# Pairwise bilinear products on one core: x transposed in pairs of fields, one buffer for 384 pairs of w, and another split of x loads between two DMA queues

## The chip, the cores and the metric

One core of a Trainium2 chip runs the kernel. The metric is the device time of one execution in microseconds (us); lower is better. Five runs of the kernel before gave 1345.14 to 1346.18 us, median 1345.78 us.

## The reference

`x` is (4096, 32, 64) in float32: 4096 samples of 32 fields with 64 numbers each. `W` is (496, 64, 64): one 64 x 64 matrix for each of the 496 pairs of fields (i, j) with i < j.

```
idx_i, idx_j = np.triu_indices(32, k=1)
vi, vj = x[:, idx_i, :], x[:, idx_j, :]
out = jnp.einsum('bpd,pde->bpe', vi, W) * vj        # (4096, 496, 64) float32
```

Field i of a sample is multiplied by the pair's matrix, and the result, element by element, by field j. The output has 520 MB, x has 33.5 MB and W has 8.1 MB.

## The kernel before

**Tiles and blocks.** A block is 256 samples, two to each of the 128 partitions (sample `k` of a partition is 0 or 1). A block has two tiles, one for each `k`, so there are 16 blocks and 32 tiles. A block of x stands in SBUF as one buffer `xs` of 1 + 64 fields to a partition (L71); field 0 is set to zero by GpSimd (L72), so that each field can be transposed with the one ahead of it. There are two such buffers, and x is loaded one block ahead.

**W.** The 496 pairs are loaded in four chunks of 128, 128, 128 and 112 pairs (L113 to L118), reordered by a copy (`order_w`, L120) and transposed on TensorE (`turn_w`, L127). They stay in SBUF as four buffers `wT`, with one half of the output columns on partitions 0 to 63 and the other half on partitions 64 to 127.

**x.** `turn_x` (L138) makes the transposed x of eight fields: eight transposes on TensorE, each of a field with the one ahead of it, into PSUM, and one ScalarE copy of 128 x 1024 to SBUF (L147). A tile needs four of them, and each is put out four steps ahead of the step that first uses it (`AHEAD`, L174).

**Steps.** A step is one field i and up to 16 of its partners j. For each chunk of w that the step touches, two matmuls (L244), one for each half of the output columns and on its own half of the partitions, write PSUM. VectorE then multiplies PSUM by the 16 partners of x (L261) and writes `ot`. For seven values of i ScalarE copies PSUM to `tmp` (L258) and GpSimd multiplies (L259).

**Output.** A tile's 496 pairs are cut in five groups of 90, 97, 99, 105 and 105 pairs. A group is one buffer `ot`, of which there are three, and one transfer on SyncE's queue (L266): 128 rows of 23,040 to 26,880 bytes. The first three tiles go group by group, since w arrives in between; from the fourth on each tile goes through its five groups.

**Loads of x.** Blocks 0 and 1 are loaded on SyncE's queue. For the others the load is put out at the seventh step of the block ahead (L188 to L191), when the last reads of the buffer's old block are done. It goes on ScalarE's queue as one transfer of 128 rows of 16 KB (L76). Blocks 4, 7, 10 and 13 go another way (`load_fifteen`, L95):

- rows 0 to 119 on GpSimd's queue in two transfers of half the fields (L103), with pieces of 4 KB;
- after each of these a small transfer of 17 rows of four bytes (`turn_engines`, L86);
- rows 120 to 127 on ScalarE's queue, in a transfer of five rows and one of three (L99), 16 KB a row.

A transfer of 120 rows on GpSimd's queue takes 15 of the core's 16 DMA engines, and the small one takes the remaining one, so that the next transfer of 120 rows leaves out the same engine. One call of `turn_engines` with five rows at the start sets which engine that is; one with eleven at the end (L270) brings the count back to a multiple of 16.

**Order.** Each engine's instructions run in the order of its queue. The order follows from the loop over the steps and from the dictionaries `due` (transposes and copies) and `loads` (x loads), which the kernel fills ahead of the loop.

Of the kernel before, what the change touches and what calls it, by code (L numbers as in the profile page):

```python
# [8 lines left out]
F32 = mybir.dt.float32  # L9
# [3 lines left out]
def kernel(  # L13
# [16 lines left out]
    nc = tc.nc  # L30

    B, F, D = x.shape
    P = 128
    NB = 2
# [3 lines left out]
    E2 = D // 2  # L38
    BANK = 512
    CH = BANK // E2  # L40
    RUN = 2 * BANK // P
    p0 = [i * (F - 1) - i * (i - 1) // 2 for i in range(F)]


# [7 lines left out]
    wrows = list(zip(cuts[:-1], cuts[1:]))  # L52

    const = ctx.enter_context(tc.tile_pool(name="const", bufs=1))
    xpool = ctx.enter_context(tc.tile_pool(name="xpool", bufs=2))
    xtpool = ctx.enter_context(tc.tile_pool(name="xtpool", bufs=4))
    tpool = ctx.enter_context(tc.tile_pool(name="tpool", bufs=4))
    opool = ctx.enter_context(tc.tile_pool(name="opool", bufs=3))
    psum = ctx.enter_context(tc.tile_pool(name="psum", bufs=4, space=bass.MemoryType.PSUM))

    ident = const.tile([P, P], F32, tag="ident", name="ident")
    make_identity(nc, ident)

    xs = {}

    def rows_of(dram: bass.AP, blk: int) -> bass.AP:
        return dram[blk * NB * P : (blk + 1) * NB * P]

    def new_x(blk: int):

        xs[blk] = xpool.tile([P, 1 + NB * F, D], F32, tag="xs", name=f"xs_{blk}")  # L71
        nc.gpsimd.memset(xs[blk][:, 0, :], 0.0)  # L72

    def load_x(blk: int, eng, k0: int = 0, k1: int = NB):
        src = rows_of(x, blk).rearrange("(p k) f d -> p (k f) d", k=NB)
        eng.dma_start(out=xs[blk][:, 1 + k0 * F : 1 + k1 * F, :], in_=src[:, k0 * F : k1 * F, :])  # L76

# [3 lines left out]
    SWR = 120  # L81
# [4 lines left out]
    def turn_engines(k: int):  # L86
        n = k if k > 1 else 17
        c = used[0] % 8
        used[0] += 1
        src = x[: NB * n].rearrange("(p k) f d -> p k f d", k=NB)  # L90
        tc.keep_in_program_order(
            nc.gpsimd.dma_start(out=scratch[:n, :, c : c + 1], in_=src[:, :, 0, 0:1])  # L92
        )

    def load_fifteen(blk: int):  # L95
        rows = rows_of(x, blk).rearrange("(p k) f d -> p k f d", k=NB)
        dst = xs[blk][:, 1:, :].rearrange("p (k f) d -> p k f d", k=NB)
        for a, b in ((SWR, SWR + 5), (SWR + 5, P)):
            nc.scalar.dma_start(out=xs[blk][a:b, 1:, :], in_=rows[a:b].rearrange("p k f d -> p (k f) d"))  # L99
        for h in range(2):  # L100
            cut = slice(h * F // 2, (h + 1) * F // 2)
            tc.keep_in_program_order(
                nc.gpsimd.dma_start(out=dst[:SWR, :, cut, :], in_=rows[:SWR, :, cut, :])  # L103
            )
            turn_engines(1)


    wflat = w.rearrange("p d e -> p (d e)")
    raw, wT = {}, {}
    EU = 2 * BANK // P  # L110
    NU = E2 // EU

    def load_w(c: int, eng=nc.sync):  # L113

        a, b = wrows[c]
        pool, tag = ((opool, "ot"), (opool, "ot"), (const, "w3"), (const, "w3"))[c]
        raw[c] = pool.tile([P, D * D], F32, tag=tag, name=f"raw_{c}")
        eng.dma_start(out=raw[c][: b - a, :], in_=wflat[a:b])  # L118

    def order_w(c: int, k: int, copy):  # L120
        r = wrows[c][1] - wrows[c][0]
        rp = tpool.tile([P, EU, 2, D], F32, tag="tmp", name=f"rp_{c}_{k}")
        src = raw[c][:r, :].rearrange("p (d h e) -> p e h d", h=2, d=D)
        copy(rp[:r], src[:, k * EU : (k + 1) * EU])  # L124
        return rp

    def turn_w(c: int, k: int, rp, copy):  # L127
        r = wrows[c][1] - wrows[c][0]
        if c not in wT:
            wT[c] = const.tile([P, r, E2], F32, tag=f"w{c}", name=f"wT_{c}")  # L130
        pt = psum.tile([P, EU, P], F32, tag="ps", name=f"ptw_{c}_{k}")
        for n in range(EU):
            nc.tensor.transpose(  # L133
                pt[:, n, :r], rp[:r, n].rearrange("p h d -> p (h d)"), ident[:r, :r]
            )
        copy(wT[c][:, :, k * EU : (k + 1) * EU], pt[:, :, :r].rearrange("p e r -> p r e"))  # L136

    def turn_x(blk: int, k: int, q: int, copy):  # L138

        pt = psum.tile([P, RUN, P], F32, tag="ps", name=f"ptx_{blk}_{k}_{q}")  # L140
        for n in range(RUN):
            s = k * F + q * RUN + n
            nc.tensor.transpose(  # L143
                pt[:, n, :], xs[blk][:, s : s + 2, :].rearrange("p f d -> p (f d)"), ident
            )
        xT = xtpool.tile([P, RUN, P], F32, tag="xT", name=f"xT_{blk}_{k}_{q}")
        copy(xT, pt)  # L147
        return xT


# [8 lines left out]
    first = {}  # L159
# [11 lines left out]
    place = {ts: n for n, ts in enumerate(sched)}  # L171


    AHEAD = 4  # L174
    due: dict = {}
    for t in range(NT):
        for q in range(F // RUN):
            at = place[t, first[q * RUN - 1] if q else 0] - AHEAD
            due.setdefault(max(0, at), []).append(("x", t // NB, t % NB, q))
    for c, orders, turns in (  # L180
# [9 lines left out]
    loads = {place[blk * NB, LATE]: blk + 1 for blk in range(2, NBLK - 1)}  # L190
    loads[place[LEAD, LATE]] = 2  # L191

    new_x(0)
    load_x(0, nc.sync, 0, 1)
    load_w(0)
    load_w(1)
    load_x(0, nc.sync, 1, NB)
    load_w(2)
    new_x(1)
    load_x(1, nc.sync)  # L200
    turn_engines(5)

    v, p, a = nc.vector.tensor_copy, nc.gpsimd.tensor_copy, nc.scalar.copy
    xT, rps = {}, {}
    xT[0, 0, 0] = turn_x(0, 0, 0, a)
    due[0] = [d for d in due[0] if d != ("x", 0, 0, 0)]
    for k, copy in enumerate((v, v, v, a)):
        rps[0, k] = order_w(0, k, copy)
    for k, copy in ((0, a), (3, a), (1, v), (2, a)):
        turn_w(0, k, rps.pop((0, k)), copy)  # L210

    ots = {}
    for s, (t, st) in enumerate(sched):
        blk, kt = divmod(t, NB)
        g, i, c0, m = steps[st]
        if s in loads:
            new_x(loads[s])
            if loads[s] % 3 == 1:
                load_fifteen(loads[s])
            else:  # L220
                load_x(loads[s], nc.scalar)
        for what, *args in due.get(s, ()):
            if what == "x":
                xT[tuple(args)] = turn_x(*args, a)
            elif what == "turn":
                turn_w(*args, rps.pop(tuple(args)), a)
            else:
                c, k = args
                rps[c, k] = order_w(c, k, (v, v, p, v)[c] if k % 2 == 0 else (v, v, p, a)[c])
                if (c, k) == (2, NU - 1):  # L230
                    load_w(3, nc.scalar)

        base, end = groups[g]
        pa = p0[i] + c0
        if pa == base:
            ots[t] = opool.tile([P, cap, D], F32, tag="ot", name=f"ot_{t}_{g}")
        ot = ots[t]
        ps = psum.tile([P, 2, CH, E2], F32, tag="ps", name=f"ps_{s}")
        for c, (lo, hi) in enumerate(wrows):
            lo, hi = max(pa, lo), min(pa + m, hi)  # L240
            if lo < hi:
                for h in range(2):
                    n = i + 1 - h
                    nc.tensor.matmul(  # L244
                        ps[:, h, lo - pa : hi - pa, :],
                        xT[blk, kt, n // RUN][h * D : (h + 1) * D, n % RUN, :],
                        wT[c][h * D : (h + 1) * D, lo - wrows[c][0] : hi - wrows[c][0], :],
                        start=True,
                        stop=True,
                    )  # L250
        o = pa - base
        j = 1 + kt * F + i + 1 + c0
        dst = ot[:, o : o + m, :].rearrange("p m (h e) -> p m h e", h=2)
        src = ps[:, :, :m, :].rearrange("p h m e -> p m h e")
        xj = xs[blk][:, j : j + m, :].rearrange("p m (h e) -> p m h e", h=2)
        if i in aside and c0 == 0 and s not in no_aside:
            tmp = tpool.tile([P, CH, 2, E2], F32, tag="tmp", name=f"tmp_{s}")
            nc.scalar.copy(tmp, src)  # L258
            nc.gpsimd.tensor_mul(dst, tmp, xj)  # L259
        else:  # L260
            nc.vector.tensor_mul(dst, src, xj)  # L261

        ends = (p0[2], end) if s < NS and (t, g) == (0, 0) else (end,)
        if pa + m in ends:
            n0 = p0[2] if len(ends) > 1 and pa + m == end else base
            nc.sync.dma_start(  # L266
                out=rows_of(out, blk).rearrange("(p k) n d -> p k n d", k=NB)[:, kt, n0 : pa + m, :],
                in_=ot[:, n0 - base : pa + m - base, :],
            )
# [28 lines left out]
```

## Time and profile before

| | |
|---|---|
| median of five runs | 1345.78 us (1345.14 to 1346.18) |
| the profiled execution | 1345.42 us, span 1343.6 us |
| moved by DMA | 562.95 MB: 520.09 MB written to HBM, 41.68 MB read |
| SyncE's DMA queue (q1), share of 16 engines | 93.0% |
| ScalarE's DMA queue (q10) | 4.2% |
| GpSimd's DMA queue (q0) | 1.5% |
| busy TensorE / VectorE / GpSimd / ScalarE | 1165.8 / 956.0 / 545.2 / 374.2 us |
| granted TensorE clock | 0.962 |

A DMA transfer is cut in packets, here one for each contiguous piece of a row, and spread over 16 DMA engines; 128 rows give each engine eight rows. Each engine ends its share with a record of four bytes, and a transfer has landed when the last of the 16 has written it. The trace holds the queue, the start, the duration and the size of every packet, but not its engine. Sorted by time, the 16 closing records of each of the 167 transfers of SyncE's queue show when the eighth engine and when the last engine were done with it.

### The profile page before, as it was taken

The page shows a single profiled execution, that of the slowest core. Times are in us where ns is not written, and L with a number is a line of the kernel's source. Part 1 is how long each engine was busy: PE and PEld are TensorE (multiplying, and loading weights), DVE is VectorE, ACT ScalarE, POOL GpSimd, SP SyncE. Part 2 cuts the span into 40 slices and gives each one's busy share as a digit, 9 for nine tenths or more (in the row PEclk, how much of TensorE's full clock was granted, in tenths as well). Part 3 has the DMA queues.
Part 4 walks back from the last instruction along what each step waited for, and adds up shares of the span by engine and source line. Part 5 has one row for each costly group of instructions (what it writes and reads, how often), then busy time and mean ns, then how long its engine had stood idle before and what let it go on. Part 6 is the DMA issues. An engine that isn't in the chain of part 4 may idle for free.

```text
span 1343.6 us, 17902 instructions
## 1 busy us (share of the span) xinstructions
PE 1165.8 (87%) x7424; PEld 680.2 (51%) x7424; DVE 956.0 (71%) x1262; ACT 374.2 (28%) x367; POOL 545.2 (41%) x264
## 2 busy tenths in 40 slices
PE   6989889888898888898889888888988889889894
PEld 4555545545455444455545554444554445545552
DVE  5778768766677677776758777576876667767774
ACT  3432222223232232232232222232222323223321
POOL 1822424444243445333444434442444424344431
PEclk9989999999999899999989999899899989989997
DMA  9999999999999999999999999999999999999997
GB/s 394 375 422 421 416 428 432 427 418 430 425 431 423 433 427 403 426 424 433 430 420 429 401 425 430 424 426 417 420 420 413 430 423 430 420 427 426 422 417 320
DMA packets 28258, 562.95 MB, mean 419 GB/s; under 512 B 3456, under 2 KB 3456, under 8 KB 5504
## 3 DMA queue, kind: packets, MB, share of 16 engines
q1 hardware_dynamic: 24048, 530.59, 93.0%
q10 hardware_dynamic: 1632, 23.33, 4.2%
q0 software_dynamic: 2496, 7.88, 1.5%
q8 instruction: 58, 0.95, 0.3%
q14 instruction: 24, 0.20, 0.0%
HBM read 41.68 MB, written 520.09 MB: 418 GB/s over the span
## 4 chain that ended last, share of the span: by engine, by line
DMA 53%; PE 22%; DVE 16%; POOL 5%; issue 2%; ACT 0%; DVEq 0%; SPq 0%; POOLq 0%; ACTq 0%
DMA out_dram<-ot 52%; PE ps L244 17%; DVE ot L261 15%; POOL ot L259 4%; PE ptx L143 4%; PE ptw L133 1%; DMA raw<-in_L_rec_W_dram 1%; POOL scratch L92 0%; ACT tmp L258 0%; DVE rp L124 0%; POOL xs L103 0%; POOL rp L124 0%; DVEq L261 0%; ACT wT L136 0%; POOLq L259 0%
## 5 line engine op out<-in xcount | busy, mean ns | idle before, releaser
L261 DVE TENSOR_TENSOR ot<-ps,xs 128x1024 f32<-128x1024 f32 (+15 forms) x1252 | 944.8, 808 | 356.7 <-DMA out_dram<-ot 187.4
L244 PE MATMUL ps<-wT,xT 64*128 64x512 f32 (+13 forms) x6272 | 1020.2, 467 | 118.6 <-DVE ot L261 106.7
L244 PEld LDWEIGHTS ps<-wT,xT 64*128 64x128 f32 x6272 | 553.4, 194 | 551.2 <-DVE ot L261 288.8
L259 POOL TENSOR_TENSOR ot<-tmp,xs 128x1024 f32<-128x1024 f32 x220 | 519.5, 2362 | 621.7 <-ACT tmp L258 436.2
L258 ACT COPY tmp<-ps 128x1024 f32<-128x1024 f32 x220 | 222.8, 1013 | 467.1 <-PE ps L244 397.6
L147 ACT COPY xT<-ptx 128x1024 f32<-128x1024 f32 x128 | 129.6, 1013 | 452.3 <-PE ptx L143 452.3
L143 PE MATMUL ptx<-ident,xs 128*128 128x128 f32 x1024 | 141.2, 281 | 37.5 <-DVE ot L261 29.1
L143 PEld LDWEIGHTS ptx<-ident,xs 128*128 128x128 f32 x1024 | 111.1, 142 | 84.1 <-issue 41.9
L72 POOL MEMSET xs<- 128x64 f32 x16 | 2.4, 152 | 148.3 <-DVE ot L261 148.3
L133 PE MATMUL ptw<-ident,rp 128*128 128x128 f32 (+1 forms) x128 | 18.6, 299 | 4.0 <-DVE rp L124 4.0
L133 PEld LDWEIGHTS ptw<-ident,rp 128*128 128x128 f32 (+1 forms) x128 | 15.7, 157 | 10.3 <-DVE rp L124 5.0
L136 ACT COPY wT<-ptw 128x1024 f32<-128x1024 f32 (+1 forms) x15 | 14.8, 984 | 20.9 <-PE ptw L133 20.9
L124 DVE COPY rp<-raw 128x1024 f32<-128x1024 f32 (+1 forms) x9 | 10.7, 1216 | 10.9 <-DMA raw<-in_L_rec_W_dram 10.9
L92 POOL DMA_DIRECT2D scratch<-in_r_inputs_dram x10 | 9.1, 908 | 0.2 <-issue 0.2
L124 POOL COPY rp<-raw 128x1024 f32<-128x1024 f32 x4 | 7.9, 1986 | 0.1
L124 ACT COPY rp<-raw 112x1024 f32<-112x1024 f32 (+1 forms) x3 | 5.9, 1955 | 4.6 <-POOL ot L259 2.8
L103 POOL DMA_DIRECT2D xs<-in_r_inputs_dram x8 | 6.0, 754 | 1.4 <-issue 1.4
L136 DVE COPY wT<-ptw 128x1024 f32<-128x1024 f32 x1 | 1.2, 1225 | 2.8 <-PE ptw L133 2.8
L147 ACT ACT_TABLE_LOAD x1 | 1.3, 1283 | 0.7 <-PEq L285 0.7
masks.py:197 POOL MEMSET ident<- 128x128 f32 x1 | 0.2, 205 | 0.3 <-POOLq L285 0.3
masks.py:199 POOL TENSOR_SCALAR_AFFINE_SELECT ident<-ident 128x128 f32<-128x128 f32 x1 | 0.3, 288 | 0.0
L285 POOL MEMSET const-float32-0.0<- 128x1 f32 x1 | 0.1, 93 | 0.3 <-issue 0.3
(3 smaller groups left out, 0.3 us busy)
## 6 DMA issues: line engine op xcount, KB each, us to landing
out_dram<-ot SPq DMA_DIRECT2D x64, 3360.0 KB, 16.3
out_dram<-ot SPq DMA_DIRECT2D x32, 3168.0 KB, 16.4
out_dram<-ot SPq DMA_DIRECT2D x32, 3104.0 KB, 17.0
out_dram<-ot SPq DMA_DIRECT2D x31, 2880.0 KB, 17.2
xs<-in_r_inputs_dram ACTq DMA_DIRECT2D x10, 2048.0 KB, 17.2
xs<-in_r_inputs_dram POOLq DMA_DIRECT2D x8, 960.0 KB, 31.7
raw<-in_L_rec_W_dram SPq DMA_DIRECT2D x3, 2048.0 KB, 17.2
xs<-in_r_inputs_dram SPq DMA_DIRECT2D x2, 1024.0 KB, 5.2
```

The costliest lines, as they stand in the source:

```text
L72: nc.gpsimd.memset(xs[blk][:, 0, :], 0.0)
L92: nc.gpsimd.dma_start(out=scratch[:n, :, c : c + 1], in_=src[:, :, 0, 0:1])
L103: nc.gpsimd.dma_start(out=dst[:SWR, :, cut, :], in_=rows[:SWR, :, cut, :])
L124: copy(rp[:r], src[:, k * EU : (k + 1) * EU])
L133: nc.tensor.transpose(pt[:, n, :r], rp[:r, n].rearrange("p h d -> p (h d)"), ident[:r, :r])
L136: copy(wT[c][:, :, k * EU : (k + 1) * EU], pt[:, :, :r].rearrange("p e r -> p r e"))
L143: nc.tensor.transpose(pt[:, n, :], xs[blk][:, s : s + 2, :].rearrange("p f d -> p (f d)"), ident)
L147: copy(xT, pt)
L244: nc.tensor.matmul(ps[:, h, lo - pa : hi - pa, :], xT[blk, kt, n // RUN][h * D : (h + 1) * D, n % RUN, :], wT[c][h * D : (h + 1) * D, lo - ...
L258: nc.scalar.copy(tmp, src)
L259: nc.gpsimd.tensor_mul(dst, tmp, xj)
L261: nc.vector.tensor_mul(dst, src, xj)
```

## The change

The diff below has all that is touched but comments.

- `xs` loses its zero field and its memset. Each partition now holds its two samples apart, with 16 unused elements behind each, so a row of 16 KB can't be one piece: every load of x is made of pieces of 8 KB.
- `turn_x` transposes fields two by two: four transposes in place of eight for eight fields. Three ScalarE copies bring the result to SBUF, one of 128 x 512 and two of 64 x 512 that swap the halves of the partitions. Each is put out six steps ahead of the step that uses field 8q, instead of four ahead of the one for field 8q - 1.
- The first three chunks of w (384 pairs) stand in one buffer, so steps that cross a border between them need one pair of matmuls instead of two.
- Blocks 3, 6, 9, 12 and 15 take `load_fifteen` in place of 4, 7, 10 and 13. It is now one transfer of 120 rows in pieces of 8 KB, one small transfer of 17 rows, and two transfers of eight rows in pieces of 4 KB, all on GpSimd's queue.

In the two programs as built, TensorE's order holds 1024 transposes of x before and 512 after, and 3136 matmuls at L244 before and 3008 after (the profile has two records for each); VectorE's has the same multiplications.

```diff
-    RUN = 2 * BANK // P
+    RUN = 8
...
     def new_x(blk: int):
-        xs[blk] = xpool.tile([P, 1 + NB * F, D], F32, tag="xs", name=f"xs_{blk}")
-        nc.gpsimd.memset(xs[blk][:, 0, :], 0.0)
+        wide = xpool.tile([P, NB, F * D + 16], F32, tag="xs", name=f"xs_{blk}")
+        xs[blk] = wide[:, :, : F * D].rearrange("p k (f d) -> p k f d", d=D)

     def load_x(blk: int, eng, k0: int = 0, k1: int = NB):
-        src = rows_of(x, blk).rearrange("(p k) f d -> p (k f) d", k=NB)
-        eng.dma_start(out=xs[blk][:, 1 + k0 * F : 1 + k1 * F, :], in_=src[:, k0 * F : k1 * F, :])
+        src = rows_of(x, blk).rearrange("(p k) f d -> p k f d", k=NB)
+        eng.dma_start(out=xs[blk][:, k0:k1], in_=src[:, k0:k1])
...
     def load_fifteen(blk: int):
         rows = rows_of(x, blk).rearrange("(p k) f d -> p k f d", k=NB)
-        dst = xs[blk][:, 1:, :].rearrange("p (k f) d -> p k f d", k=NB)
-        for a, b in ((SWR, SWR + 5), (SWR + 5, P)):
-            nc.scalar.dma_start(out=xs[blk][a:b, 1:, :], in_=rows[a:b].rearrange("p k f d -> p (k f) d"))
+        dst = xs[blk]
+        def part(ps: slice, fs: slice):
+            tc.keep_in_program_order(nc.gpsimd.dma_start(out=dst[ps, :, fs, :], in_=rows[ps, :, fs, :]))
+        part(slice(0, SWR), slice(0, F))
+        turn_engines(1)
         for h in range(2):
-            cut = slice(h * F // 2, (h + 1) * F // 2)
-            tc.keep_in_program_order(
-                nc.gpsimd.dma_start(out=dst[:SWR, :, cut, :], in_=rows[:SWR, :, cut, :])
-            )
-            turn_engines(1)
+            part(slice(SWR, P), slice(h * F // 2, (h + 1) * F // 2))
...
     def turn_w(c: int, k: int, rp, copy):
-        if c not in wT:
-            wT[c] = const.tile([P, r, E2], F32, tag=f"w{c}", name=f"wT_{c}")
+        home, tag, n = (wrows[c][0], "w3", r) if c == 3 else (0, "w", wrows[3][0])
+        if home not in wT:
+            wT[home] = const.tile([P, n, E2], F32, tag=tag, name=f"wT_{home}")
...
     def turn_x(blk: int, k: int, q: int, copy):
-        pt = psum.tile([P, RUN, P], F32, tag="ps", name=f"ptx_{blk}_{k}_{q}")
-        for n in range(RUN):
-            s = k * F + q * RUN + n
+        pt = psum.tile([P, RUN // 2, P], F32, tag="ps", name=f"ptx_{blk}_{k}_{q}")
+        for u in range(RUN // 2):
+            f = q * RUN + 2 * u
             nc.tensor.transpose(
-                pt[:, n, :], xs[blk][:, s : s + 2, :].rearrange("p f d -> p (f d)"), ident
+                pt[:, u, :], xs[blk][:, k, f : f + 2, :].rearrange("p f d -> p (f d)"), ident
             )
-        xT = xtpool.tile([P, RUN, P], F32, tag="xT", name=f"xT_{blk}_{k}_{q}")
-        copy(xT, pt)
+        xT = xtpool.tile([P, 2, RUN // 2, P], F32, tag="xT", name=f"xT_{blk}_{k}_{q}")
+        copy(xT[:, 0], pt)
+        copy(xT[D:, 1], pt[:D])
+        copy(xT[:D, 1], pt[D:])
         return xT
...
-    AHEAD = 4
+    AHEAD = 6
...
-            at = place[t, first[q * RUN - 1] if q else 0] - AHEAD
+            at = place[t, first[q * RUN]] - AHEAD
...
-            if loads[s] % 3 == 1:
+            if loads[s] % 3 == 0:
                 load_fifteen(loads[s])
...
-        for c, (lo, hi) in enumerate(wrows):
-            lo, hi = max(pa, lo), min(pa + m, hi)
+        for lo, hi in ((0, wrows[3][0]), wrows[3]):
+            home, lo, hi = lo, max(pa, lo), min(pa + m, hi)
             if lo < hi:
                 for h in range(2):
-                    n = i + 1 - h
                     nc.tensor.matmul(
                         ps[:, h, lo - pa : hi - pa, :],
-                        xT[blk, kt, n // RUN][h * D : (h + 1) * D, n % RUN, :],
-                        wT[c][h * D : (h + 1) * D, lo - wrows[c][0] : hi - wrows[c][0], :],
+                        xT[blk, kt, i // RUN][h * D : (h + 1) * D, (i + h) % 2, i % RUN // 2, :],
+                        wT[home][h * D : (h + 1) * D, lo - home : hi - home, :],
```

More of the change, by code (lines that the diff above doesn't have):

```diff
@@ L135, in turn_w @@
             )
-        copy(wT[c][:, :, k * EU : (k + 1) * EU], pt[:, :, :r].rearrange("p e r -> p r e"))
+        o = wrows[c][0] - home
+        copy(wT[home][:, o : o + r, k * EU : (k + 1) * EU], pt[:, :, :r].rearrange("p e r -> p r e"))
     def turn_x(blk: int, k: int, q: int, copy):
-        pt = psum.tile([P, RUN, P], F32, tag="ps", name=f"ptx_{blk}_{k}_{q}")
-        for n in range(RUN):
-            s = k * F + q * RUN + n
+        pt = psum.tile([P, RUN // 2, P], F32, tag="ps", name=f"ptx_{blk}_{k}_{q}")
+        for u in range(RUN // 2):
+            f = q * RUN + 2 * u
             nc.tensor.transpose(
-                pt[:, n, :], xs[blk][:, s : s + 2, :].rearrange("p f d -> p (f d)"), ident
+                pt[:, u, :], xs[blk][:, k, f : f + 2, :].rearrange("p f d -> p (f d)"), ident
             )
-        xT = xtpool.tile([P, RUN, P], F32, tag="xT", name=f"xT_{blk}_{k}_{q}")
-        copy(xT, pt)
+        xT = xtpool.tile([P, 2, RUN // 2, P], F32, tag="xT", name=f"xT_{blk}_{k}_{q}")
+        copy(xT[:, 0], pt)
+        copy(xT[D:, 1], pt[:D])
+        copy(xT[:D, 1], pt[D:])
         return xT
@@ L251 @@
         o = pa - base
-        j = 1 + kt * F + i + 1 + c0
+        j = i + 1 + c0
         dst = ot[:, o : o + m, :].rearrange("p m (h e) -> p m h e", h=2)
         src = ps[:, :, :m, :].rearrange("p h m e -> p m h e")
-        xj = xs[blk][:, j : j + m, :].rearrange("p m (h e) -> p m h e", h=2)
+        xj = xs[blk][:, kt, j : j + m, :].rearrange("p m (h e) -> p m h e", h=2)
         if i in aside and c0 == 0 and s not in no_aside:
```

## The prediction

> **What bounds the kernel now.** I read the page first: the DMA row, the shares of the chain that ended last, and then who waits for whom.
>
> ```profile
> DMA  9999999999999999999999999999999999999997
> ...
> DMA packets 28258, 562.95 MB, mean 419 GB/s; under 512 B 3456, under 2 KB 3456, under 8 KB 5504
> ...
> DMA 53%; PE 22%; DVE 16%; POOL 5%; issue 2%; ACT 0%; DVEq 0%; SPq 0%; POOLq 0%; ACTq 0%
> ```
>
> The 16 DMA engines are busy in every slice, and transfers are over half of the chain. The waits (total us, times, longest) say what compute lacks:
>
> ```profile
> POOL ot L259 <- DMA out_dram<-ot: 161.9, 69, 5.5
> ...
> DVE ot L261 <- DMA out_dram<-ot: 187.4, 92, 5.6
> ```
>
> VectorE and GpSimd wait for an output buffer whose transfer hasn't landed. The end of the chain (start, us, what) shows the same; the last transfer, issued at 1326.37, starts where it stops:
>
> ```profile
> 1279.13 16.21 DMA out_dram<-ot
> ...
> 1301.17 17.05 DMA out_dram<-ot
> 1318.23 0.03 issue
> 1318.26 0.05 DVEq L261
> 1318.31 0.04 issue
> 1318.35 7.86 DVE ot L261 x13
> ```
>
> So DMA is the bound; the question is which part of it. I sorted the closing records of each transfer (16, one to an engine):
>
> ```
> bytes a row  issued   8th done  last done  last - last of the transfer ahead
> 26880        463.07    473.29    478.54     8.27
> 26880        471.58    481.24    486.75     8.21
> 23040        477.90    488.06    493.81     7.06
> 24832        484.90    495.41    501.42     7.61
> 25344        493.31    502.91    509.21     7.79
> ...
> 26880       1326.37   1335.29   1341.50     7.95
> ```
>
> **One engine is late, and has no gaps.** Over such undisturbed stretches the last record comes every 38.98 us per tile (five transfers), the eighth every 37.61: one engine moves 26.05 bytes/ns, the middle one 27.0. At 111.41 us all 16 close within 0.20 us; from there to 1341.50 the others are held back by buffers the late one hasn't freed, and end 5 to 6 us ahead of it. If it never idles, its work is the time. Its 150 transfers hold 30.53 MB: at 26.05 bytes/ns 1172 us. Around each load of x the last record comes later than this by:
>
> - ten loads on ScalarE's queue: 4.70 to 4.77 us each, sum 47.4;
> - four through `load_fifteen`: 3.17, 2.65, 2.68, 2.60, sum 11.1.
>
> 1172 + 58.5 = 1230.5 us, and 1341.50 - 111.41 is 1230.1. The late engine's work explains the whole time behind the start.
>
> **Loads of x: the term that counts.** On a transfer of 120 rows the late engine gets no x: GpSimd's queue shows 4-byte packets at 516.07, 517.12, 518.16, 519.19, 520.19 us and on, the spacing of its own output packets (1.03 us), in place of pieces of 4 KB. So what does a `load_fifteen` still cost it? At 511 us ScalarE's five rows begin, and the late engine's next transfer is 0.68 us longer: one row of 16 KB (611 ns a packet, times 27.0/26.05 = 633). The other 2.0 us fall on the two transfers of 120 rows with the two small ones: 1.0 us for a pair. After the change:
>
> - One pair remains, with pieces twice as large and so the same 16 to an engine: 1.0 us.
> - The eight rows take eight engines in each half, 16 in the two, so the late one has one row-half: two 4 KB packets of 159 ns, 0.33 us, and some 0.1 us of closing. The row of 16 KB is gone.
> - Sum 1.45 us. It can't be below 0.33 + 0.1 = 0.4, and I see nothing that would make it dearer than the 2.78 us (11.1 / 4) of now.
> - A load on ScalarE's queue in pieces of 8 KB: packets of 8,192 bytes have a median of 309 ns, two are 618 against 611; eight rows make 0.06 us. 4.74 + 0.06 = 4.80 us. Below this: nothing, since the bytes stay.
>
> After: 9 x 4.80 + 5 x 1.45 = 50.45 us. Before: 58.5. **Difference -8.05 us**; with the bounds 0.4 and 2.78 it is -13.3 to -1.4. I take 1.45, which is made of rows of these very transfers.
>
> For the engines at full speed the new split is dearer: 32 pieces of 159 ns are 5.09 us, eight packets of 611 are 4.89. They end 5 us ahead, so that is covered; without the cover it would be 0.05 to 0.2 us a load. Here the Trainium skill speaks against the change: "DMA: Bandwidth & Descriptors", Issuing engine by pattern, sends a simple load to SyncE and calls that queue type generally faster than GpSimd's. The packet rows agree, and by them a fifth block on GpSimd's queue costs 0.2 us where by the late engine it saves 3.3; the sum would be +0.2 instead of -8.05.
>
> **Is the late engine late early enough?** The first such load moves from block 4 (264 us) to block 3 (181.7 us). A saving there counts only if the engine has work waiting. From 111.41 to 208.26 its bytes and two loads make 87.3 + 9.4 = 96.7 us, the records 96.85: it is busy. Put 3.3 us ahead it would begin the transfer issued at 208.88 near 212.6, still after its issue. I count the saving in full; lost, it is 3.3 us.
>
> **GpSimd's and ScalarE's queues.** GpSimd issued four transfers for such a block (2 x 754 and 2 x 908 ns, 3.3 us) and issues four after, so five blocks cost it 16.6 in place of 13.3 us. Behind them stands its multiply L259, for which it is idle 621.7 us in all. ScalarE drops two issues of 257 to 511 ns. The 16 memsets (152 ns) go; their wait for VectorE (148.3 us, GpSimd otherwise idle) becomes the wait of the load itself, on ScalarE's or GpSimd's queue, for the same last reads. Behind it stand L259 and ScalarE's copies L258, as now. Zero; if exposed, under 1 us a block.
>
> **x transposes.** Rows: L143 x1024, 281 ns, or 1.09 us for eight; L147 x128, 1013 ns. After: 4 x 128 transposes, 0.55 us a group, so 512 fewer, some 70 us of TensorE. ScalarE's 128 x 896 copy takes 906 ns and its 128 x 1024 one 1012, 0.83 ns an element, so a 512 copy is about 0.60; three are 1.8, and 128 x 0.8 = 100 us are added to its 374.2. Both lie under the DMA: compute alone fills five buffers in 34.5 to 36.7 us (issue less the later of the issue ahead and the landing of the buffer's old content), against 38.98 + 50.45/30 = 40.7 after. Four groups a tile with 0.8 us more each, all on the path, less nothing for TensorE, make 39.9: still covered. The PSUM buffer is held 0.25 us longer (1.8 + 0.55 against 1.01 + 1.09). Zero.
>
> **One buffer for 384 pairs.** 128 matmuls fewer (256 records at L244, 467 ns the mean of all); TensorE waits 288.8 us for VectorE already. Zero behind 111 us.
>
> **The start.** Up to 111.41 us compute sets the pace and nothing hides it. `AHEAD` 6 puts the second sample's transposes in front of the first matmul (18.57 us); their x lands at 18.26, then 0.55: 0.3 us late. Block 1's stand in front of the seventh step's matmul, where TensorE arrives near 26.1 (two thirds through the twelve matmuls that begin at 24.29), and that x lands at 28.04: some 2 us of standing, of which 1.0 is regained, since the transposes once behind (28.93, 1.09 us) are gone. Against this, five groups between 58 and 103 us are 0.5 us shorter each. I take 0, from -2 to +1.5.
>
> **Sum.** 1345.42 - 8.05 = 1337.4 for the profiled execution, which stands 0.36 below the median: **1337.7**.
>
> **Rivals.**
>
> - *The cheap load isn't cheaper on the late engine* (pieces of 8 KB are cut in two, or the small transfer is the cost). Cut in two, the pair costs 1.5 us instead of 1.0 and the gain is 5.5: 1340.2. At 2.78 us a load it is 1.4 and the time 1344.4, no change that shows. For it: I infer the share from spacing, not from an engine's name.
> - *The first relief is wasted*: the late engine, put ahead at 190 us, idles. 3.3 us less: 1341.0. Against it: the queue stood 10 us deep at the transfer issued at 197.95, whose predecessor ended at 208.26.
> - *The start gets slower* by its 1.5 us: 1339.2.
> - *Slower: the wrong engine is spared.* The change does what it says only if the four transfers (15, 1, 8 and 8 engines) move GpSimd's queue on by a multiple of 16. If the two of eight rows do otherwise, from the second load on the late engine gets 16 pieces of 8 KB at 0.32 us, 5.1, beside the rest: 43.2 + 1.45 + 4 x 5.5 = 66.7, +8.2 us: 1354. Against it: before, 15 + 1 held its place over four loads.
>
> **How the numbers follow.** Forecast (near 1337.7, the slower start within it) 0.60; pieces cut in two 0.12; first relief wasted 0.08; no cheaper load 0.11; wrong engine, or compute exposed, 0.09. A measurement of this kernel can tell about 0.2% (2.7 us) from no change, so faster is below 1343.1: 0.60 + 0.12 + 0.08 = 0.80; same 0.11; slower 0.09. The range: below, the loads at 1.0 us each and a start 1.5 us quicker give 1334; above, 1344.4 takes in all but the slower case.
>
> **What would show it.** Right: the last records still 38.98 us a tile apart; 1.45 us more than that around blocks 3, 6, 9, 12 and 15, 4.8 around the others; the last engine's lead over the eighth smaller after 181 us; 4-byte packets 1.03 us apart, 16 in each. Wrong: 4 KB packets from the 120 rows; the last engine in step with the eighth (then the others or compute bind); waits of VectorE for TensorE or of L259 for ScalarE grown beyond what the waits for `out_dram` lose.

## The result, and the profile after

The changed kernel takes **1343.12 us** (median of 30 runs, 1341.32 to 1345.51), the one before 1345.76 us (median of the 50 runs beside them). The ratio is 0.9981, with a 95% interval of 0.9976 to 0.9986. The gain is 2.6 us, 0.19%, where 8.05 us were predicted: it is small, but a ratio of 1 lies outside the interval. The profiled execution took 1343.31 us, its span is 1341.5 us.

The page of the kernel after: the DMA row, its packets, the queues (packets, MB, share of 16 engines), the chain of work that ended last, and the group of the transposes (busy, mean ns of one, idle time ahead and its releaser).

```profile
DMA  9899999999999999999999999999999999999997
...
DMA packets 28894, 562.86 MB, mean 420 GB/s; under 512 B 3536, under 2 KB 3536, under 8 KB 3824
...
q1 hardware_dynamic: 24176, 530.59, 93.0%
q10 hardware_dynamic: 2576, 20.71, 3.8%
q0 software_dynamic: 2064, 10.50, 2.0%
...
DMA 59%; PE 21%; DVE 13%; POOL 4%; issue 2%; ACT 1%; SPq 0%; DVEq 0%; POOLq 0%; ACTq 0%
...
L146 PE MATMUL ptx<-ident,xs 128*128 128x128 f32 x512 | 84.5, 288 | 12.2 <-DMA xs<-in_r_inputs_dram 9.6
```

DMA is still the bound, and more of the chain is transfers. The x bytes went from ScalarE's queue (q10) to GpSimd's (q0) as the change says, and the second slice of the DMA row has an 8 now: in the start the engines stand. The last row says for whom: the transposes wait 9.6 us for x, in three waits. In the kernel before it was one (total us, times, longest):

```profile
PE ptx L143 <- DMA xs<-in_r_inputs_dram: 6.1, 1, 6.1
```

So the first wait, for the first x of the program, is old, and some 3.8 us in two waits are new. The waits for an output buffer have not shrunk (total us, times, longest):

```profile
DVE ot L265 <- DMA out_dram<-ot: 205.8, 97, 6.6
...
POOL ot L263 <- DMA out_dram<-ot: 185.9, 72, 7.3
```

VectorE waits 18 us more and GpSimd 24 us more than before, while their busy times hardly moved (956.0 to 953.6 and 545.2 to 543.3 us). The chain of waits ends as before, on a transfer and the last 13 multiplications, 2.2 us earlier:

```profile
1299.07 17.00 DMA out_dram<-ot
1316.07 0.03 issue
1316.10 0.05 DVEq L265
1316.15 0.04 issue
1316.19 7.86 DVE ot L265 x13
```

So the answer lies in the transfers. Their closing records, sorted as in the prediction, split the profiled time in two:

```
                                      before    after
first full-size transfer, last close  111.41    113.98
from there to the last close         1230.09   1225.37
last transfer: 8th engine closes     1335.29   1333.39
               15th                  1336.46   1336.65
               16th                  1341.50   1339.35
```

The start lost 2.57 us, and the stretch behind it gained 4.72 us instead of 8.05. At the end the 15th engine is 2.7 us ahead of the last one instead of 5.0. And behind the loads through `load_fifteen` the last closing records can keep the pace of the others: from 470.98 to 508.55 us, one tile, they are 37.57 us apart instead of 38.98. By the prediction that would be a sign that the late engine no longer sets the time.

### The profile page after: what moved, and what is told of

It reads as the page before. It is cut to its first block, busy times and chain, and to the rows that moved or that the text cites. A ratio compares the mean times of both kernels' runs of the same rounds, so it can differ in the third digit from the quotient of the medians.

```text
span 1341.5 us, 16676 instructions
## 1 busy us (share of the span) xinstructions
PE 1140.7 (85%) x6656; PEld 605.0 (45%) x6656; DVE 953.6 (71%) x1262; ACT 468.0 (35%) x623; POOL 543.3 (40%) x252
## 4 chain that ended last, share of the span: by engine, by line
DMA 59%; PE 21%; DVE 13%; POOL 4%; issue 2%; ACT 1%; SPq 0%; DVEq 0%; POOLq 0%; ACTq 0%
DMA out_dram<-ot 57%; PE ps L248 18%; DVE ot L265 12%; POOL ot L263 4%; DMA xs<-in_r_inputs_dram 2%; PE ptx L146 2%; ACT tmp L262 1%; PE ptw L134 1%; DVE rp L124 0%; POOL rp L124 0%; DVEq L265 0%; POOL xs L100 0%; SPq L118 0%; ACT xT L150 0%; ACT xT L151 0%
## 5 line engine op out<-in xcount | busy, mean ns | idle before, releaser
L248 PE MATMUL ps<-wT,xT 64*128 64x512 f32 (+13 forms) x6016 | 1049.3, 489 | 166.0 <-DVE ot L265 161.4
L248 PEld LDWEIGHTS ps<-wT,xT 64*128 64x128 f32 x6016 | 535.1, 196 | 621.4 <-DVE ot L265 374.8
L150 ACT COPY xT<-ptx 128x512 f32<-128x512 f32 x128 | 75.0, 586 | 321.4 <-PE ptx L146 321.4
L146 PE MATMUL ptx<-ident,xs 128*128 128x128 f32 x512 | 84.5, 288 | 12.2 <-DMA xs<-in_r_inputs_dram 9.6
L146 PEld LDWEIGHTS ptx<-ident,xs 128*128 128x128 f32 x512 | 54.0, 141 | 85.2 <-DVE ot L265 60.3
L152 ACT COPY xT<-ptx 64x512 f32<-64x512 f32 x128 | 74.6, 582 | 1.6
L151 ACT COPY xT<-ptx 64x512 f32<-64x512 f32 x128 | 73.9, 577 | 1.5
L100 POOL DMA_DIRECT2D xs<-in_r_inputs_dram x15 | 9.5, 635 | 0.0
L92 POOL DMA_DIRECT2D scratch<-in_r_inputs_dram x7 | 6.2, 889 | 0.3 <-issue 0.3
## 6 DMA issues: line engine op xcount, KB each, us to landing
xs<-in_r_inputs_dram SPq DMA_DIRECT2D x2, 1024.0 KB, 10.4
```

What stands on the lines that cost most here:

```text
L100: tc.keep_in_program_order(nc.gpsimd.dma_start(out=dst[ps, :, fs, :], in_=rows[ps, :, fs, :]))
L146: nc.tensor.transpose(pt[:, u, :], xs[blk][:, k, f : f + 2, :].rearrange("p f d -> p (f d)"), ident)
L150: copy(xT[:, 0], pt)
L151: copy(xT[D:, 1], pt[:D])
L152: copy(xT[:D, 1], pt[D:])
L248: nc.tensor.matmul(ps[:, h, lo - pa : hi - pa, :], xT[blk, kt, i // RUN][h * D : (h + 1) * D, (i + h) % 2, i % RUN // 2, :], wT[home][h * ...
```

## How the late engine's own work was read

The trace names no engine, but its packets can be linked: on one engine a packet begins 3 to 4 ns before the end of the one ahead (now and then 13 ns, and around packets of four bytes up to 20 ns from it). In undisturbed stretches 15 engines move 26,880 bytes in 996 ns, and one takes mostly 1,010 to 1,060 ns; from there its chain can be followed, with the order of row sizes of the transfers as a check. It goes from the late engine's first closing record of a full-size transfer (111.33 us before, 113.98 after) to the last one of the program without a gap of more than 20 ns, and it holds the packets of x that the loads must give it: 84 of 16 KB before; 144 of 8 KB and ten of 4 KB after. So this engine never idles, also where another one closes a transfer last. What a load takes beyond the output bytes at 26.05 bytes/ns is what it costs the late engine (us):

```
                                      before             after
the chain in all                      1230.2             1225.4
its output bytes at 26.05 bytes/ns    1172.1             1172.1
loads on ScalarE's queue              47.4 (10 of them)  42.2 (9)
loads through load_fifteen            10.4 (4)           11.5 (5)
rest                                   0.2               -0.4
one load on ScalarE's queue           4.67 to 4.88       4.63 to 4.82 (predicted 4.80)
one through load_fifteen              2.49 to 2.66       2.12 to 2.62 (predicted 1.45)
```

The rest says how far such an account closes: to some 0.6 us here.

In the load of block 6 the late engine of the kernel after does this (start us, queue, bytes, ns):

```
441.837 q1 26880 1028      448.033 q1 23040 1313
442.858 q1 26880 1042      449.345 q0     4    7
443.897 q0     4    9      449.358 q1 23040 1025
443.903 q1 26880 1000      450.386 q0     4    7
...                        450.400 q1 23040 1078
445.777 q1 23040 1032      451.479 q0     4    7
446.811 q0     4    7      451.491 q1 23040 1032
446.824 q1 23040 1187      452.521 q0     4    7
448.015 q0     4    7      452.526 q1 23040 1106
```

It gets four-byte packets in place of pieces of x, as predicted, but while the other fifteen read, seven of its output packets of 23,040 bytes take 1025 to 1313 ns, where 884 would be 26.05 bytes/ns. These are 1.6 us, five times what its two pieces of 4 KB take (0.32 us). In all five loads the longer output packets make 1.6 to 2.0 us; the four-byte packets, at 6 to 9 ns each, make some 0.2.

## The experiments

The theory after the result: the late engine's work is still the time, but a load through `load_fifteen` costs it 2.3 us, and the start is 2.6 us later because TensorE stands for x. The rivals: another engine has taken over as the last one, or the price is one for each transfer.

**start4**: the order of the start undone.

```diff
-            at = place[t, first[q * RUN]] - AHEAD
+            at = place[t, first[q * RUN]] - (4 if t < LEAD else AHEAD)
```

> The kernel after, with AHEAD 4 for the first three samples only: TensorE does two steps of matmuls before it stands for the transposes of the second sample and of block 1. Theory (the start is a term of its own: TensorE's 2.98 us of standing at 24.9 us): the first full-size transfer closes at 111.4 us again instead of 113.98, and the whole time falls by the same 2.6 us, from 1343.1 to 1340.5. Rival (the start is regained behind, because the DMA queue sets the end from wherever it begins): 1343 +- 0.5.

Measured: 1340.16 us, ratio to the kernel before 0.9964 (0.9952 to 0.9976). That is 2.96 us less than the kernel after; the start's loss is not regained behind it. TensorE's timeline of the kernel after (start us, us, engine, line, operation; in brackets the idle time ahead and what ended it):

```profile
18.05 0.63 PE L146 MATMUL ptx<-ident,xs 128*128 128x128 f32 x4 [0.81 <-DMA xs<-in_r_inputs_dram]
...
23.10 1.83 PE L248 MATMUL ps<-wT,xT 64*128 64x512 f32 x8
27.91 0.63 PE L146 MATMUL ptx<-ident,xs 128*128 128x128 f32 x4 [2.98 <-DMA xs<-in_r_inputs_dram]
28.46 1.47 PE L248 MATMUL ps<-wT,xT 64*128 64x512 f32 x4
```

of the kernel before at the same place:

```profile
24.29 2.69 PE L244 MATMUL ps<-wT,xT 64*128 64x512 f32 x12
26.91 1.09 PE L133 MATMUL ptw<-ident,rp 128*128 128x128 f32 x8
27.93 1.07 PE L244 MATMUL ps<-wT,xT 64*128 64x480 f32 x4
28.93 1.09 PE L143 MATMUL ptx<-ident,xs 128*128 128x128 f32 x8
```

and of start4:

```profile
23.42 2.69 PE L248 MATMUL ps<-wT,xT 64*128 64x512 f32 x12
26.04 1.09 PE L134 MATMUL ptw<-ident,rp 128*128 128x128 f32 x8
27.06 1.08 PE L248 MATMUL ps<-wT,xT 64*128 64x480 f32 x4
28.07 0.66 PE L146 MATMUL ptx<-ident,xs 128*128 128x128 f32 x4
```

With block 1's transposes in front, TensorE has nothing to do from 24.93 to 27.91 us; with a lead of four steps instead of six it fills that time with the twelve matmuls, a group of w and four more matmuls, as in the kernel before, and the transposes find their x there. The eighth engine closes the ninth transfer at 41.85 us instead of 46.31.

**no_relief**: every load on ScalarE's queue (`if loads[s] < 0:` in place of `% 3 == 0`).

> The kernel after, with every load of x on ScalarE's queue, none through load_fifteen. Price of one load_fifteen on the late engine: by the prediction 1.45 us against 4.80, so five of them gone cost 5 x 3.35 = 16.8 us: 1359.9. By the records of the kernel after, about 2.2 us: 5 x 2.65 = 13.3: 1356.4. If half of the relief is wasted because another engine is last in many stretches: 1350 or less.

Measured: 1353.31 us, 1.0059 (1.0047 to 1.0071): 10.2 us above the kernel after, 2.0 for each load. That is nearer to the records' 13.3 than to the prediction's 16.8, and below both; the late engine's chain is 11.7 us longer than in the kernel after (1237.1 us, 65.2 of them for the fourteen loads).

**wrong_one**: the other engine spared.

```diff
-    turn_engines(5)
+    turn_engines(6)
...
-    turn_engines(11)
+    turn_engines(10)
```

> The kernel after with the first tiny transfer one row longer (turn_engines(6)) and the last one a row shorter, so that the engine that gets no rows of a 120-row load is the next one. If one engine is late and the change spares it: the five loads cost it 5.3 us or more in place of 2.3, as if they were not there or worse: 1354 to 1359. If it matters little which one is spared: 1343.

Measured: 1357.75 us, 1.0089 (1.0075 to 1.0103), 14.6 us above the kernel after with the same loads; the five now cost the late engine 5.25 to 5.37 us each. There is one late engine, and the change spares the right one: the slower rival of the prediction is refuted.

**no_third**: block 3 on ScalarE's queue too (`if loads[s] % 3 == 0 and loads[s] > 3:`).

> The kernel after, with block 3 loaded on ScalarE's queue and only blocks 6, 9, 12, 15 through load_fifteen. If the first such load counts like the others (no_relief: 10.2 us for five): 2.0 to 2.3 us more, 1345.3. If it is wasted, because the late engine had hardly fallen behind by 182 us: 1343.1 +- 0.5.

Measured: 1345.67 us, 0.9996 (0.9987 to 1.0005), 2.55 us above the kernel after. The first such load counts like the others; that rival falls as well.

**eight_whole**: the late engine gets no piece of x at all.

```diff
-        for h in range(2):
-            part(slice(SWR, P), slice(h * F // 2, (h + 1) * F // 2))
+        part(slice(SWR, P), slice(0, F))
+        turn_engines(8)
```

> The kernel after, but the last eight rows in one transfer (engines 0 to 7 behind the pair) and a tiny transfer of eight rows behind it for the other eight engines, so that the late engine, at place 15, gets no piece of x at all. If its two 4 KB packets (0.33 us) are part of its price: 5 x 0.33 = 1.7 us less, 1341.5. If its price is in the four closings and the small packets: 1343.1 +- 0.4. If another engine is the last one now (the eight engines now get 16 KB more each instead of 8): up to 0.3 us a load slower, 1344.6.

Measured: 1341.19 us, 0.9964 (0.9951 to 0.9977), 1.9 us less than after; by the linked packets the five loads cost the late engine 9.9 us instead of 11.5 (2.70 for the first, then 1.65 to 1.92). The difference is five times its two 4 KB packets (0.31). They are a real part of its price, and the rest, some 1.9 us, is not x of its own.

**two_pairs**: the 120 rows in two transfers again.

```diff
-        part(slice(0, SWR), slice(0, F))
-        turn_engines(1)
+        for h in range(2):
+            part(slice(0, SWR), slice(h * F // 2, (h + 1) * F // 2))
+            turn_engines(1)
```

> The kernel after, but the 120 rows in two transfers (halves of the fields, 4 KB pieces), each with its small one: the pairs of the kernel before. The prediction had 1.0 us on the late engine for each pair, so one more pair costs 5 x 1.0 = 5 us: 1348. Theory of now: what the late engine loses in such a load beside its own pieces (2.3 us less 0.4) comes once a load, while the other fifteen engines read, however the 120 rows are cut: 1343.1 +- 0.8.

Measured: 1343.54 us, 0.9982 (0.9973 to 0.9991): no different from the kernel after. A pair has no price of its own: the five loads cost the late engine 11.0 us, 1.92 to 2.66 each. The prediction's "1.0 us for a pair" divided by two what comes once a load. Linked, the kernel before already shows it: of its four loads the first pair costs the late engine 0.03 to 0.40 us, the second 1.6 to 1.8.

**half_read**: half the bytes.

```diff
-        part(slice(0, SWR), slice(0, F))
+        nc.gpsimd.memset(dst[:SWR, :, F // 2 :, :], 0.0)
+        part(slice(0, SWR), slice(0, F // 2))
```

> The kernel after, but the 120 rows of the five loads bring only the first half of the fields (half the bytes, 4 KB pieces); GpSimd writes zeros to the other half, so this part of x is left out. The late engine has no piece of these rows in either case. If what it loses beside its own pieces (some 1.9 us a load) lasts as long as the other fifteen read: half of it goes, 5 x 0.95 = 4.7 us, 1338.4. If it is a fixed price of the four transfers and their closings: 1343.1 +- 0.8. (The full-speed engines have 2.5 us less a load in either case.)

Measured: 1333.22 us, 0.9900 (0.9885 to 0.9915), 9.9 us less than after, twice what was expected. By the linked packets its loads cost the late engine 0.40 to 0.46 us (the first 0.88), 2.5 us in all and 9.0 less than in the kernel after: that is nearly the whole difference. What is left is its own two pieces (0.31) and, but for the first load, hardly more; in those four loads its 23,040-byte packets take 855 to 934 ns among as many four-byte ones. So without the other half of the bytes the loss is gone, not halved. What is left out here is always the second half of the fields, which in the kernel before and in spaced is the dear one, so the run does not show that the loss goes with the number of bytes.

**spaced**: all the bytes, in two stretches 24 steps apart.

```diff
+        if s in second:
+            load_fifteen(second[s], 1)
...
-                load_fifteen(loads[s])
+                load_fifteen(loads[s], 0)
+                second[s + 24] = loads[s]
```

`load_fifteen(blk, h)` issues half h of the 120 rows with its small transfer, and the eight rows with the second half.

> two_pairs with 24 steps (some 20 us) between the two pairs of a load; the eight rows go with the second. In the kernel after the late engine's own output packets take 1.5 to 2.1 us longer in each such load, mostly in its second half; with half the bytes (half_read) 0 to 0.4. If that comes of the length of one stretch in which the fifteen read, two separate halves cost 0.3 each: 5 x 1.4 = 7 us less, 1336. If it comes of the bytes: as two_pairs, 1343.5.

Measured: 1342.72 us, 0.9975 (0.9965 to 0.9985). The 5 us or more of the first theory don't come. The late engine's price is 1.84 to 2.23 us a load, 10.4 in all, its chain has no gap, and the account closes (1172.1 + 42.2 + 10.4 = 1224.7 us): its work is still the time. Up to the end of the first half a load costs it -0.1 to 0.0 us, in the second half 1.5 to 1.8 beside its own pieces. So the length of one stretch isn't the cause: a half that stands alone is free, and the other one, 20 us later, has the whole price. In two_pairs, with no steps between, the first half costs 0.02 to 0.91 us and the second most of the rest, so it is not strictly the second either. Whether the fields that are read, the order, or what is written meanwhile makes the one half dear was not tried.

**relief_all**: all fourteen loads through `load_fifteen` (`if loads[s] > 0:`).

> The kernel after, with all fourteen loads of x through load_fifteen. Theory A (the slow engine's work is the time up to the end): nine more loads at 2.2 us instead of 4.85: 24 us less, 1319; the engines at full speed would need 1131 + 14 x 5.15 = 1203 us from 114 us on, so they bind at about 1321. Theory B (with five such loads a second engine at full rate is already the last one in many stretches, and each further load costs it 5.1 in place of 4.85): 1343 to 1346.

Measured: 1344.01 us, 0.9988 (0.9976 to 1.0001). Nine more relieved loads bring nothing: of the 24 us of theory A none come, and theory B's 1343 to 1346 holds. Behind the loads the last closing records come in steps of 7.95, 6.82, 7.35, 7.50 and 7.95 us, 37.57 a tile: a full-speed engine is the last one, not the late one with its 38.98. Such steps are in the kernel after too; but here the late engine's chain breaks off, and it waits for work. From the first full-size transfer to the end it needs 1229.1 us, 98 beyond its output bytes at 27.0, or 7.0 us a load, where its own pieces of x take 16 x 0.309 + 0.32 = 5.3. The page shows how full the engines are:

```profile
DMA  8999999999999999999999999999999999999998
...
q1 hardware_dynamic: 24176, 530.59, 93.2%
q0 software_dynamic: 5664, 29.40, 5.3%
q10 hardware_dynamic: 128, 1.84, 0.4%
```

93.2 + 5.3 + 0.4 are 98.9% of all 16 engines' span. That alone does not tell the two theories apart, since it was 98.7% in the kernel before (93.0 + 4.2 + 1.5).

**best5** and **best7**: start4 and eight_whole in one, with five loads relieved or seven (`% 2 == 1`).

> start4 and eight_whole in one, five loads through load_fifteen as in the change. If the start and the late engine's pieces are terms that add up: 1343.1 - 3.0 - 1.9 = 1338.2. If the engines at full speed take over once the late one is relieved further: no better than start4 or best7, 1339.5 or more.

> start4 and eight_whole in one, and load_fifteen for blocks 3, 5, 7 .. 15 (seven). If the late engine's work is still the time: 1343.1 - 2.6 (start) - 1.9 (eight rows) - 2 x (4.6 - 1.9) = 1333.2. If the engines at full speed bind (relief_all: 1229 us from the first full-size transfer to the end with fourteen, 8th engine 1226): about 1338, no better than start4 and eight_whole together.

Measured: 1339.08 us, 0.9946 (0.9933 to 0.9958), and 1339.53 us, 0.9952 (0.9939 to 0.9964). These are the fastest versions, 7.2 and 6.4 us below the kernel before. The sum of the two parts would be 1338.2. In best5 the late engine's chain still has no gap (1222.6 us, 8.6 of them for the five loads), so its work is the time; in best7 it has gaps, and seven relieved loads add nothing to five, as the full-speed engines' bound said. In both, the two last engines end within 1.1 us of each other (1335.68 and 1336.73, 1336.24 and 1336.35).

**spaced5** and **spaced7**: the same with the two stretches.

> spaced with start4 and eight_whole, five such loads. If the stretch counts: best5's 1339.1 less 5 us, 1334. If the engines at full speed bind already in best5: 1338 to 1339.

> spaced5 with seven such loads (blocks 3, 5 .. 15). If the late engine binds in spaced5: 2 x (4.7 - 0.6) = 8 us less than it, 1326. If the engines at full speed bind: within 1 us of spaced5.

Measured: 1340.36 us, 0.9965 (0.9953 to 0.9977), and 1341.92 us, 0.9974 (0.9963 to 0.9986). The late engine pays 0.9 to 1.2 us for four of spaced5's loads, less than in best5 (1.5 to 1.7), and still nothing is won: in both runs its chain has gaps. The full-speed engines bind.

**old_loads** and **old_16k**: the kernel after with the loads of before (blocks 4, 7, 10, 13, two pairs, five and three rows on ScalarE's queue), in pieces of 8 KB or, without the pad, in rows of 16 KB.

> The kernel after, with the loads of before (blocks 4, 7, 10, 13; two pairs of transfers, the eight rows as five and three on ScalarE's queue). What is left of the change is TensorE's transposes by 16, the copies, one w buffer, no memsets and the later start. Theory (only the start and the loads count): 2.6 us above the kernel before, 1348.4. Rival (the lighter TensorE or fewer memsets is worth something behind the start): 1346 or less.

> old_loads with every load on ScalarE's queue in rows of 16 KB (no pad of 16 elements), so that all loads are as in the kernel before and only transposes, copies, the w buffer, the memsets and the start differ from it. old_loads was 1345.35, though its start is 3 us later. If the pieces of 8 KB are what brought these 3 us back (0.12 us less on each of ten loads, and 0.3 to 0.6 less for the last eight rows on each of four): 1348.4. If the lighter TensorE, the memsets or something else did: 1345.4.

Measured: 1345.35 us, 0.9997 (0.9988 to 1.0006), and 1344.30 us, 0.9985 (0.9977 to 0.9994). This missed: with nothing changed but transposes, copies, buffers and the start, old_16k is faster than the kernel before. Pieces of 8 KB are not the reason, since the version with them is the slower one. Its records show the start 1.5 us later (112.88) and the rest 3.2 us shorter (1226.9). The late engine's chain (1227.3 us) does not put that to the four loads through `load_fifteen`: they cost 10.2 us, against 10.4 for the same transfers in the kernel before. Of the difference 0.4 us are in the ten loads on ScalarE's queue and 2.3 in the output outside the loads, which this engine writes at 26.11 bytes/ns instead of 26.04. What makes it do so is open. old_loads pays the same for its loads (46.9 and 9.8 us), and its start takes away what it gains.

## Why the prediction was wrong, step by step

- **"One pair remains ... 1.0 us", and so "Sum 1.45 us"**: this step failed. It read the late engine's time in a load as a price for each pair of transfers. It is time that its own output packets lose while fifteen engines read (eight_whole, two_pairs, half_read), and one pair brings all of it: 2.1 to 2.6 us a load, 11.5 us for five instead of 7.25. The relief of a fifth block is then eaten by its own price: 11.5 against 10.4 before. What remains of the saving is the load that left ScalarE's queue and a little from the others there (42.2 us against 47.4). What makes the packets longer stays open. The reading of 3.17 us for the first load before also held 0.7 us that are not this load's on the late engine, 0.3 of them a packet of another queue; linked, the load cost 2.49.
- **The start, "I take 0, from -2 to +1.5"**: this step failed too. Its mechanism was right, down to the place (the seventh step's matmul); the size was not. TensorE stood 2.98 us instead of "some 2", since its matmuls ahead were done by 24.93 us and not near 26.1, and nothing of it came back: 2.57 us by the records, 3.0 by start4.
- **The late engine's work is the time**: right for the kernels before and after: its chain has no gap in either, nor in any run but relief_all, best7, spaced5 and spaced7, and wrong_one, eight_whole and no_third move the time by what they do to this engine. The prediction's sign against it, a last record in step with the others, misled: in the kernel after the late engine is up to 2.9 us ahead of the last one behind such loads and still has work waiting.
- **"They end 5 us ahead, so that is covered"**: right for five loads, and the cover is thinner than it looked. The others lose up to 7.0 us a load (relief_all), and they are last once the late engine is relieved by 5 us more than in the kernel after (spaced5: 6.4 us for its five loads; with 8.6, in best5, they are not). The sum beside it was too low as well: its 32 pieces of 4 KB, 5.09 us, are the split of the kernel before, and the new one gives such an engine 16 of 8 KB and two of 4 KB, 5.26.
- **Loads on ScalarE's queue**: 0.06 us was added to 4.74 for pieces of 8 KB. Linked, the median went from 4.74 to 4.67; the nine loads took 42.2 us instead of 43.2.
- **The first relief counts**: right; 2.55 us (no_third) instead of 3.3.
- **Compute, copies, one w buffer at zero**: no wait on them shows, but old_16k is 1.9 us faster than the kernel before. Most of that is in the late engine's output outside the loads; how the edits reach it was not found.
- **GpSimd's queue against the rule of the Trainium skill** ("DMA: Bandwidth & Descriptors", Issuing engine by pattern: a simple load belongs to SyncE): up to five blocks GpSimd's queue wins here, 10.2 us against no_relief, because its transfer can leave one engine out. Nine more blocks on it bring nothing beyond that (relief_all).

With what was measured in place of the prediction's terms the sum is -8.05 + 4.25 (11.5 for 7.25) + 2.57 (start) - 1.0 (42.2 for 43.2) = -2.2 us, against -2.1 in the profiled execution and -2.6 between the medians.

## What to carry to other kernels

A price that was read from one form of transfer may belong to the event and not to the transfer: before halving it, find a run or a stretch where the one changes and the other doesn't. Here the rows of the kernel before had it: its two pairs of a load did not cost the same. An engine that is spared work only helps until the next ones are last, so work out their time as well, with what they pay beside their own bytes. And where the start has no cover, a lead of a few steps more is no free edit: compare the landing of each operand with the moment at which the engine is done with what stands ahead.

## What the runs showed of the hardware

One of the 16 DMA engines is slow in the kernels before and after and in every run whose chain can be followed to the end (all but relief_all, best7, spaced5 and spaced7): 26.05 bytes/ns in undisturbed stretches (26.11 in old_16k) against 27.0. wrong_one shows that it is the one at the same place of GpSimd's queue in all five loads.

The four-byte packets that it gets in place of x cost 6 to 9 ns each, some 0.2 us a load. Where they take 7 ns instead of 9, the output packets between them are mostly the long ones, in the load shown 1025 to 1313 ns. This is a tendency and no rule: in the kernel after the rows behind 7-ns packets are 19% longer in the median, and 27% of those behind 9-ns ones are more than 3% longer too. Whether one causes the other was not tried. In loads on ScalarE's queue, where this engine reads its own share, its output packets stay at 26.05 bytes/ns or slightly above.

The Trainium skill ("DMA: Bandwidth & Descriptors", Latency and other measured facts) says that engines 7 and 15 are usually slower than the others, and guesses that all engines' fetching of the software queue's descriptors crowds a port that these two use. The longer packets of the loads on GpSimd's queue, and none on ScalarE's, agree with that. half_read, with as many pieces (of half the size) and hardly longer packets, and the first pairs of the kernel before do not, and the 26.05 bytes/ns of stretches in which GpSimd's queue moves nothing are not explained by it. No run here tells the number of the late engine.

Up to 111 us compute sets the pace, and the profiled execution of best5 lost there what start4 had kept: its first full-size transfer closed at 115.52 us instead of 111.73. Half of that comes with a lower granted clock. The stretches of start4 and then of best5 (stretch, its length, busy time of each engine, granted clock, DMA share, GB/s), each with the same twelve matmuls:

```profile
80.00:86.00 6.00, 6.00 (x35) 4.12 (x34) 3.52 (x5) 2.65 (x4) 0.00 (x0) 0.73 0.98 417
86.00:90.00 4.00, 4.00 (x30) 2.49 (x29) 3.42 (x5) 1.16 (x2) 0.00 (x0) 1.00 1.04 446
...
83.53 2.05 PE L248 MATMUL ps<-wT,xT 64*128 64x288 f32 x12
```

```profile
80.00:86.00 6.00, 6.00 (x22) 3.56 (x24) 3.72 (x5) 2.09 (x4) 0.00 (x0) 0.50 1.00 425
86.00:90.00 4.00, 4.00 (x18) 2.05 (x17) 2.17 (x3) 0.56 (x1) 0.00 (x0) 0.57 1.00 431
...
85.50 3.89 PE L248 MATMUL ps<-wT,xT 64*128 64x288 f32 x12
```

At 0.50 and 0.57 the twelve matmuls took 3.89 us instead of 2.05. The other 2.0 us stood before them, and 1.4 of these already at the ninth transfer, whose eighth engine closed at 43.27 us instead of 41.85 with the clock at 1.00 in both. A single profile says little about a start of this kind; the medians of start4 and the kernel after carry that verdict.
